# A graph layer on one core: the short slot of the scan moved to tenth place, finer last shares, a shared last normalisation

## The chip, the cores and the metric

The kernel runs on one core of one Trainium2 chip. The core has a matrix engine (TensorE, PE in the profile, with its weight loads as PEld), three engines for elementwise work (VectorE, DVE; ScalarE, ACT; GpSimd, POOL), a queue for transfers (SyncE, SP) and 16 DMA engines that all queues share. Each engine executes its own instructions in the order of the built program, and waits at an instruction until what that one needs is there. The metric is the device time of one execution in microseconds.

## What is computed

```python
def _L0_gnn_ref(x, src, dst, theta_w, theta_b, phi_w, phi_b):
    x_src = x[src]
    x_dst = x[dst]
    theta_x = (x_dst - x_src) @ theta_w.T + theta_b
    phi_x = x_src @ phi_w.T + phi_b
    e = jax.nn.relu(theta_x + phi_x)
    out = jax.ops.segment_max(e, dst, num_segments=x.shape[0])
    return jnp.where(jnp.isfinite(out), out, 0.0)
x = _layernorm(x + _L0_gnn_ref(...), axis=-1)
```

x has 6250 rows of 256 numbers; there are 100,000 edges, sorted by dst. Since relu and the maximum commute with what depends on dst alone, the kernel forms b = x @ (phi - theta).T once for each row, takes for each destination the maximum of b over its sources, adds x @ theta.T and the biases, applies relu, adds x and normalises each row.

## The kernel before

The destinations are split in two parts. Part 1 (the first 1130 nodes) is done by gathering: GpSimd gathers rows of b by edge, VectorE forms running maxima, and the results are stored in a table in device memory, maxima_1. Part 2 is the other 5120 nodes, 40 columns ("tiles") of 128. It is done in two ways at once, and this is the long stage of the kernel.

*The scan.* The 6250 rows of b are cut into 17 slots of up to 383 rows; the last slot has only 122. Each slot is applied to five chunks of 1024 nodes; a pair (slot, chunk) is a part, and there are 85. For a part, SyncE loads a row `want` (L1061, tile pool of 2) that says which row of the slot each node has chosen; VectorE builds the 0/1 mask `hot` for the slot's first block of 128 rows (L1065) and ScalarE those for the other blocks (L1067, L1068); TensorE multiplies the slot's rows (`terms`, a high and a low part) with the masks (L1075), in two halves of one PSUM tile each (`ps_f`, 3 tiles); VectorE takes the maximum into `acc` (L1086), once for each half. A slot of 383 rows has 3 blocks, so 24 matmuls of 512 columns for a part. The short slot has one block, so 8 matmuls, one mask built on VectorE, none on ScalarE, and as before two maxima.

*The list.* Edges that the scan doesn't cover are put in a list. GpSimd gathers their rows of b in 29 groups of 8 steps (gather_2, L512, a tile ring `g` of six), with a pause (L488) after each gather. All of GpSimd's gathers are held in the order in which the code calls them (`in_turn`). VectorE runs through each group with 8 dependent steps (L688), and SyncE stores each group into a second table, maxima_2 (L696).

*The order of the two.* The main loop (L1420 on) takes one list group per turn and calls scan parts (`fetch_parts`) until the blocks that are left fall below a line that SPREAD sets. Within an engine, the order that the code gives is only a priority: a scheduler, working from its own estimates of time while the program is built, lets an instruction go ahead of earlier ones that it believes to be waiting. Exceptions are GpSimd's gathers and, for most of the loop, the L688 steps, which are held behind the latest maximum of the scan (`latest_part`).

*The early share.* A share is a group of up to 8 columns of nodes that is finished together: its x rows are loaded, its maxima gathered (rows_of), TensorE multiplies x with theta, VectorE adds (L1310 for part 2 alone, L1311, L1314), then `normalise` forms the moments on ScalarE (L1328), a small chain on VectorE and a root on ScalarE (L1333, L418 to L424, L1335), scales on ScalarE (L1338) and stores (L1344). One share, LAST, holds the 106 nodes that are left over in part 1: one column. It needs nothing of the list or of the scan's part 2, and is called in the main loop in the turn of list group 26 (L1435 to L1439).

*The end.* After the loop come the 8 other columns of part 1 as one share, then the 40 columns of part 2: four shares of 8 and two of 4. The gathers for part 2 read maxima_2 and wait for all its stores. The pool of the moments `r` has 2 buffers.

Of the kernel before, what the change touches and what calls it, by code (L numbers as in the profile page):

```python
# [40 lines left out]
FP = mybir.dt.float32  # L41
I32 = mybir.dt.int32
# [4 lines left out]
AF = mybir.ActivationFunctionType  # L47
ALU = mybir.AluOpType
# [4 lines left out]
P = 128  # L53
BIG2 = 3.0e38
EPS = 1e-5
STEPS = 8
# [3 lines left out]
TILES = 40  # L60
# [4 lines left out]
KB = 3  # L65
SLOT = 512
DVE_HOTS = 1
SPREAD = 0.97
PAUSE = 160
CHOICE_R = 24  # L70
X_AFTER = 6
# [9 lines left out]
LIST_GROUPS = (LIST + STEPS - 1) // STEPS  # L81
BACK = 34
PAD_WORD = 63 << 14
CARRY_GROUPS = 5
CARRY_AT = 9
FAR = 1000000.0
GENERAL_STEPS = 17
LOWEST = -1.0e30
# [339 lines left out]
def gnn_kernel(ctx: ExitStack, tc: tile.TileContext, x, src, dst, theta_w, theta_b, phi_w, phi_b, out):  # L428
    nc = tc.nc
# [246 lines left out]
    last = {1: None, 2: None}  # L676
    latest_part = [None]

    def run(part, g, n, caps, t0, to, gathers=(), carry_row=None):


        for k in range(n):
            t = t0 + k if part == 1 else LIST_CHUNK - 1 - t0 - k
            if last[part] is not None:
                if t < 0:
                    one = nc.vector.tensor_tensor(g[:, k, :], last[part], carry_row, op=ALU.max)
                else:
                    one = nc.vector.scalar_tensor_tensor(  # L688
                        g[:, k, :], last[part], caps[:, t : t + 1], g[:, k, :], op0=ALU.min, op1=ALU.max
                    )  # L690
                if k < len(gathers):
                    behind_in_order(one, gathers[k], "rows that are there")
                if part == 2 and latest_part[0] is not None:
                    behind_in_order(one, latest_part[0], "VectorE's order")
            last[part] = g[:, k, :]
        nc.sync.dma_start(to, g[:, :n, :])  # L696

    def run_1(i, gathers=()):
        t0, n = groups[i]
# [411 lines left out]
    def list_chunks(ps):  # L1111

        upper_end, scratch, up = (src_w.bitcast(FP)[:, i * P : (i + 1) * P] for i in range(2, 5))
        nc.vector.tensor_copy(upper_end, ps[:, :P])
        nc.vector.tensor_tensor(before, ps[:, P : P + 1], n_list, op=ALU.subtract)
        chunk_0 = work.tile([P, 1], FP, name="chunk_0")
        iota(chunk_0, 0, -BACK, LIST_CHUNK)
        number = work.tile([P, 3], FP, name="number", bufs=1)
        at_edge = chunk_0
        for i in range(3):  # L1120
            nc.vector.tensor_scalar(
                scratch, upper_end, at_edge, None, op0=ALU.is_le, op1=ALU.add, accum_out=number[:, i : i + 1]
            )
            if i == 0:
                nc.vector.tensor_tensor(up, scratch, upper_end, op=ALU.mult)
                nc.vector.tensor_reduce(ends[:, 0:1], up, AX.X, ALU.max)
            nc.vector.scalar_tensor_tensor(up, scratch, FAR, upper_end, op0=ALU.mult, op1=ALU.add)
            nc.vector.tensor_reduce(ends[:, i + 1 : i + 2], up, AX.X, ALU.min)
            at_edge = ends[:, i + 1 : i + 2]
        nc.vector.tensor_scalar(ends, ends, chunk_0, 512.0, op0=ALU.subtract, op1=ALU.min)  # L1130
        nc.vector.scalar_tensor_tensor(number, number, float(OWN_LIST), ends[:, :3], op0=ALU.mult, op1=ALU.subtract)
        nc.vector.tensor_scalar(
            run_start, number, float(OWN_LIST), float((P + 2) * OWN_LIST), op0=ALU.add, op1=ALU.min
        )
        nc.vector.tensor_scalar(bad[:, 7:8], ends[:, 3:4], float(BACK + LIST_CHUNK), None, op0=ALU.is_lt)
        nc.vector.tensor_scalar(bad[:, 8:9], upper_end[:, P - 1 :], float(P * LIST_CHUNK), None, op0=ALU.is_gt)

    def list_places():

        has = work.tile([P, TILES], FP, name="has")  # L1140
        nc.vector.tensor_tensor(has, up_to[:, 1:], up_to[:, :TILES], op=ALU.is_gt)
        place_f = work.tile([P, TILES], FP, name="place_f")
        nc.vector.tensor_scalar(place_f, up_to[:, 1:], before, -1.0, op0=ALU.add, op1=ALU.add)
        chunk_of = work.tile([P, TILES], FP, name="chunk_of")
        floor_of(chunk_of, place_f, LIST_CHUNK)
        nc.vector.tensor_scalar(place_f, up_to[:, :TILES], before, None, op0=ALU.add)
        nc.vector.scalar_tensor_tensor(
            place_f, chunk_of, -float(LIST_CHUNK), place_f, op0=ALU.mult, op1=ALU.add
        )
        step = work.tile([P, TILES], I32, name="step")  # L1150
        group = work.tile([P, TILES], I32, name="group")
        nc.vector.tensor_scalar(
            group, place_f, -float(BACK), None, op0=ALU.is_lt, op1=ALU.add, accum_out=bad[:, 6:7]
        )
        apart = work.tile([P, TILES], FP, name="apart")
        nc.vector.tensor_scalar(apart, place_f, 0.0, float(1 - STEPS), op0=ALU.is_lt, op1=ALU.mult)
        nc.vector.tensor_scalar(apart, apart, float(STEPS), None, op0=ALU.add)
        nc.vector.tensor_scalar(place_f, place_f, -1.0, -1.0, op0=ALU.max, op1=ALU.mult)
        nc.vector.tensor_scalar(step, place_f, float(LIST_CHUNK - 1), 0.0, op0=ALU.add, op1=ALU.max)
        nc.vector.tensor_scalar(group, step, STEPS_BITS, None, op0=ALU.logical_shift_right)  # L1160
        nc.vector.scalar_tensor_tensor(place_f, group, float((P - 1) * STEPS), step, op0=ALU.mult, op1=ALU.add)
        nc.vector.tensor_tensor(chunk_of, chunk_of, apart, op=ALU.mult)
        nc.vector.scalar_tensor_tensor(place_f, chunk_of, 1.0, place_f, op0=ALU.add, op1=ALU.add)
        nc.vector.tensor_tensor(place_f, place_f, has, op=ALU.mult)
        nc.vector.tensor_scalar(place_2, place_f, float(P * LIST), None, op0=ALU.min)

    def list_pieces():
# [35 lines left out]
            nc.vector.copy_predicated(done[:, :n], moves[:, :n], done[:, shift : shift + n])  # L1203
            yield
        done = done[:, :OWN_LIST]
        owner = work.tile([P, 1], I32, name="owner")
        nc.gpsimd.iota(owner, pattern=[[0, 1]], base=0, channel_multiplier=1 << 20)
        nc.vector.tensor_scalar(done, done, (1 << 20) - 1, None, op0=ALU.bitwise_and)
        nc.vector.tensor_tensor(done, done, owner.to_broadcast([P, OWN_LIST]), op=ALU.bitwise_or)
# [28 lines left out]
    def list_carry():  # L1238

        nodes = wide[:, : BACK + LIST_CHUNK]  # L1240
        same = work.tile([P, BACK], FP, name="same_node")
        n_same = work.tile([P, 3], FP, name="n_same")
        nc.vector.tensor_scalar(
            same, nodes[:, :BACK], nodes[:, BACK : BACK + 1], None, op0=ALU.is_equal, op1=ALU.add, accum_out=n_same[:, 0:1]
        )
        step = work.tile([P, 1], I32, name="carry_step")
        group = work.tile([P, 1], I32, name="carry_group")
        nc.vector.tensor_scalar(step, n_same[:, 0:1], -1.0, 0.0, op0=ALU.add, op1=ALU.max)
        nc.vector.tensor_scalar(group, step, STEPS_BITS, None, op0=ALU.logical_shift_right)
        nc.vector.scalar_tensor_tensor(  # L1250
            n_same[:, 1:2], group, float((P - 1) * STEPS), step, op0=ALU.mult, op1=ALU.add
        )
        chunk_1 = work.tile([P, 1], FP, name="chunk_1")
        iota(chunk_1, 0, 1 - STEPS, STEPS)
        nc.vector.tensor_tensor(n_same[:, 1:2], n_same[:, 1:2], chunk_1, op=ALU.add)
        nc.vector.tensor_scalar(n_same[:, 2:3], n_same[:, 0:1], 0.0, None, op0=ALU.is_gt)
        nc.vector.tensor_tensor(n_same[:, 1:2], n_same[:, 1:2], n_same[:, 2:3], op=ALU.mult)
        nc.vector.tensor_scalar(carry_at, n_same[:, 1:2], 0.0, None, op0=ALU.max)
# [14 lines left out]
    def rows_of(part, j0, n, ps_tile):  # L1273
# [8 lines left out]
        maxima, places = (maxima_1, place_1) if part == 1 else (maxima_2, place_2)  # L1282
        for k in range(n):
            gather(m[:, k, :], maxima, places[:, j0 + k : j0 + k + 1])
        totals = work.tile([P, STEPS], FP, name="totals", bufs=3)

        def piece(k):
            w = min(2, n - k)
# [31 lines left out]

    def normalise(part, j0, n, x_f, totals):

        r = work.tile([P, 5, STEPS], FP, name="r")
        mean, var, root, inv, step = (r[:, k, :n] for k in range(5))
        nc.vector.tensor_scalar(mean, totals[:, :n], -1.0 / D, None, op0=ALU.mult)
        for k in range(n):
# [8 lines left out]
        nc.vector.tensor_tensor(mean, mean, inv, op=ALU.mult)  # L1335
        yield
        for k in range(n):
            nc.scalar.activation(  # L1338
                x_f[:, k, :], x_f[:, k, :], AF.Identity, bias=mean[:, k : k + 1], scale=inv[:, k : k + 1]
            )  # L1340
            if k % 2 and k + 1 < n:
                yield
        share = part, j0, n
# [30 lines left out]
                self.step()  # L1374


    parts = [(s, c) for s in range(NS) for c in range(CHUNKS)]
    groups_1 = list(range(X_GROUPS, len(groups)))
    todo = list(range(NT1))

# [41 lines left out]
    for i in range(LIST_GROUPS):  # L1422
# [3 lines left out]
            carry_row = gather_carry()  # L1426
        g, gathers = gather_2(i * STEPS)
        if i:
            run(2, g_before, STEPS, caps_2, (i - 1) * STEPS, maxima_2t[i - 1], gathers)
        g_before = g  # L1430
        while parts and blocks_left() > all_blocks * (1.0 - (i + 1) / (SPREAD * n_groups)):
            fetch_parts(1)
# [12 lines left out]

    ps_end = body.enter_context(tc.tile_pool(name="ps_end", bufs=6, space=PSUM))
    last_shares = [(2, j, STEPS) for j in range(0, TILES - STEPS, STEPS)]
    last_shares += [(2, j, STEPS // 2) for j in (TILES - STEPS, TILES - STEPS // 2)]
    at_end = Shares(lambda: ps_end.tile([P, 2 * D], FP, name="ps_e"))
    for share in [(1, 0, Q1)] + last_shares:  # L1450
        at_end.add(*share)
# [35 lines left out]
```

## Time and profile before

| what | value |
|---|---|
| median of 3 runs (lowest to highest) | 749.13 us (747.54 to 750.01) |
| the profiled execution: time, span | 746.02 us, 744.2 us |
| granted TensorE clock over the span | 0.955 |
| busy share of the span: PE, DVE, ACT, POOL | 87%, 86%, 66%, 81% |
| L1075, matmuls of the scan | x1960, 458.0 us busy |
| L1086, maxima of the scan on VectorE | x160, 193.5 us busy, 1215 ns each |
| L688, steps on gathered rows on VectorE | x376, 180.0 us busy, 479 ns each |
| L512, list gathers on GpSimd | x232, 235.4 us busy, 1015 ns each |
| L488, pauses on GpSimd | x384, 120.4 us busy, 314 ns each |
| L1338, scaling on ScalarE | x49, 25.3 us busy |

A busy share is a mean over stages that have different limits: until about 200 us the tables are prepared, then the scan and the list run together until about 655, then the shares are finished. A matmul's record overlaps with the next one's, so a busy PE is not PE at its peak. What a row of the timeline shows after its names in square brackets is how long the engine had been idle before it, and what ended that idle time.

### The profile page before, as it was taken

Reading aid. Unit: us, or ns where it says so; the run is one execution under the profiler, and the core shown is the slowest. Engines: PE = TensorE matmul, PEld = TensorE weight load, DVE = VectorE, ACT = ScalarE, POOL = GpSimd, SP = SyncE. Lnnn points to the kernel's source line nnn. Section 1 sums busy time; section 2 is a strip of 40 time slices with the busy share of each in tenths; the row PEclk is TensorE's granted clock in tenths of the full one; section 3 lists DMA queues with packets and bytes.
Section 4 is the critical chain, followed back from the end, with each engine's and each line's share of the span. In section 5 each row is a group of like instructions: output and inputs, shape, how many; then the busy total and the mean of one; then the engine's idle time right before and its main releaser. Section 6 shows DMA issues by size and latency. Waiting matters only on the chain.

```text
span 744.2 us, 10255 instructions
## 1 busy us (share of the span) xinstructions
PE 650.4 (87%) x3018; PEld 537.3 (72%) x3018; DVE 641.4 (86%) x1197; ACT 492.7 (66%) x700; POOL 604.9 (81%) x843
## 2 busy tenths in 40 slices
PE   1299999939777999999999999999999999589970
PEld 0288888726556788688888888888888888479970
DVE  6699999999997989598889989889799899768871
ACT  0144444459997777688777877877787775037885
POOL 7788987788887778888888888888888888648840
PEclk9599999959999999999999999999999999999995
DMA  6577745584677787968777777768768777625542
GB/s 207 144 244 244 248 159 193 176 286 151 209 239 256 239 254 231 356 211 267 230 235 223 261 243 251 228 223 251 262 205 261 229 222 250 224 101 180 180 173 116
DMA packets 55895, 164.84 MB, mean 221 GB/s; under 512 B 11835, under 2 KB 19796, under 8 KB 48500
## 3 DMA queue, kind: packets, MB, share of 16 engines
q1 hardware_dynamic: 32344, 98.76, 38.1%
q0 software_dynamic: 20944, 57.62, 27.5%
q10 hardware_dynamic: 2540, 7.69, 2.9%
q8 instruction: 27, 0.44, 0.3%
q14 instruction: 40, 0.33, 0.1%
HBM read 101.08 MB, written 63.74 MB: 221 GB/s over the span
## 4 chain that ended last, share of the span: by engine, by line
PE 52%; ACT 11%; DVE 5%; DMA 5%; POOL 3%; issue 2%; DVEq 0%; ACTq 0%; POOLq 0%; SPq 0%
PE ps_f L1075 49%; DMA want<-chosen_rows 4%; POOL g L512 3%; ACT x_f L1338 3%; ACT squares L1328 3%; ACT hot L1067 2%; ACT hot L1068 2%; DVE acc L1086 2%; PE ps_e L1299 1%; ACT acc L1084 1%; DMA g<-b_rows,src 1%; ACT x_t L1294 1%; DVE g L688 1%; DVE x_f L1314 1%; DVE g L1310 0%
## 5 line engine op out<-in xcount | busy, mean ns | idle before, releaser
L1075 PE MATMUL ps_f<-hot,terms 128*128 128x512 f32 x1960 | 458.0, 395 | 29.0 <-ACT hot L1068 15.6
L1075 PEld LDWEIGHTS ps_f<-hot,terms 128*128 128x128 f32 x1960 | 370.2, 190 | 113.1 <-ACT hot L1068 19.8
L512 POOL DMA_INDIRECT g<-b_rows,list_src x232 | 235.4, 1015 | 39.4 <-issue 35.6
L1067 ACT ACTIVATE hot<-want,minus_row 128x1024 fp32r<-128x1024 f16 x169 | 186.2, 1147 | 92.7 <-PE ps_f L1075 80.2
L1086 DVE TENSOR_TENSOR acc<-acc,ps_f 128x1024 f32<-128x1024 f32 x160 | 193.5, 1215 | 31.9 <-PE ps_f L1075 31.0
L688 DVE SCALAR_TENSOR_TENSOR g<-g,caps 128x256 f32<-128x256 f32 x376 | 180.0, 479 | 8.4 <-DMA g<-b_rows,src 5.2
L1068 ACT ACTIVATE hot<-hot 128x1024 fp32r<-128x1024 f32 x169 | 169.1, 1046 | 0.0
L512 POOL DMA_INDIRECT g<-b_rows,src x98 | 128.0, 1306 | 30.5 <-issue 25.3
L488 POOL IOTA pause<- 128x160 f32 x384 | 120.4, 314 | 5.5
L759 PE MATMUL ps_b<-weights,x_t 128*128 128x256 f32 x388 | 90.5, 388 | 1.3 <-ACT x_t L749 0.5
L759 PEld LDWEIGHTS ps_b<-weights,x_t 128*128 128x128 f32 x388 | 72.9, 192 | 14.4 <-ACT x_t L749 5.0
L512 POOL DMA_INDIRECT g<-in_x_dram,src x48 | 60.3, 1256 | 11.3 <-issue 7.1
L512 POOL DMA_INDIRECT g<-maxima,place x49 | 47.6, 972 | 24.6 <-issue 22.5
L1065 DVE TENSOR_SCALAR hot<-want,row_id 128x1024 fp32r<-128x1024 f16 x76 | 59.8, 788 | 6.4 <-DMA want<-chosen_rows 6.3
L1299 PE MATMUL ps_e<-weights,x_t 128*128 128x256 f32 x192 | 48.5, 380 | 0.3 <-ACT x_t L1294 0.2
L1299 PEld LDWEIGHTS ps_e<-weights,x_t 128*128 128x128 f32 x192 | 32.8, 190 | 3.9 <-ACT x_t L1294 0.8
L1294 ACT COPY x_t<-ps_e 128x512 f32<-128x512 f32 x24 | 13.7, 574 | 32.4 <-PE ps_e L1292 32.4
L762 ACT COPY b_sb<-ps_b 128x512 f32<-128x512 f32 (+1 forms) x25 | 14.4, 578 | 29.8 <-PE ps_b L759 28.0
L762 ACT COPY g<-ps_b 128x512 f32<-128x512 f32 x24 | 14.1, 586 | 29.8 <-PE ps_b L759 27.5
L1338 ACT ACTIVATE x_f<-x_f,r 128x256 f32<-128x256 f32 x49 | 25.3, 590 | 10.8 <-DVE r L1335 10.7
L749 ACT COPY x_t<-ps_xt 128x512 f32<-128x512 f32 (+1 forms) x49 | 26.1, 593 | 0.0
L1328 ACT ACTIVATE squares<-x_f,r 128x256 bf16<-128x256 f32 x49 | 24.2, 499 | 1.6 <-DMA g<-b_rows,list_src 1.0
(266 smaller groups left out, 502.2 us busy)
## 6 DMA issues: line engine op xcount, KB each, us to landing
maxima<-g SPq DMA_DIRECT2D x47, 1024.0 KB
want<-chosen_rows SPq DMA_DIRECT2D x85, 256.0 KB
x_q<-in_x_dram SPq DMA_DIRECT2D x12, 512.0 KB
b_rows<-b_sb ACTq DMA_DIRECT2D x12, 512.0 KB
x_f<-in_x_dram SPq DMA_DIRECT2D x5, 1024.0 KB
out_dram<-x_f SPq DMA_DIRECT2D x5, 1024.0 KB
raw<-b_rows SPq DMA_DIRECT2D x16, 256.0 KB
g<-b_rows,list_src POOLq DMA_INDIRECT x232, 4.3
```

The costliest lines, as they stand in the source:

```text
L488: return nc.gpsimd.iota(t, pattern=[[step, t.shape[1]]], base=base, channel_multiplier=per_partition, allow_small_or_imprecise_dtypes=True,)
L512: in_turn(nc.gpsimd.indirect_dma_start(out=out, out_offset=out_offset, in_=in_, in_offset=in_offset))
L688: one = nc.vector.scalar_tensor_tensor(g[:, k, :], last[part], caps[:, t : t + 1], g[:, k, :], op0=ALU.min, op1=ALU.max)
L759: nc.tensor.matmul(ps[:, h, :], x_t[:, h, k, :], weights[:, k, 0, :], start=(k == 0), stop=(k == KC - 1))
L1065: nc.vector.tensor_scalar(hot[:, b, :], want, row_id[:, b : b + 1], None, op0=ALU.is_equal)
L1067: nc.scalar.activation(hot[:, b, :], want, AF.Abs, bias=minus_row[:, b : b + 1], scale=1.0)
L1068: nc.scalar.activation(hot[:, b, :], hot[:, b, :].bitcast(FP), AF.Relu, bias=1.0, scale=-1.0)
L1075: nc.tensor.matmul(ps[:, w : w + 512], terms[:, part, b, h * P : (h + 1) * P], hot[:, b, w : w + 512], start=(i == 0), stop=(i == n - 1),)
L1086: latest_part[0] = nc.vector.tensor_tensor(to, to, ps, op=ALU.max).ins.name
L1299: nc.tensor.matmul(a[:, i, :], x_t[:, 2 * i + c, :], weights[:, c, 1, :], start=(c == 0), stop=False)
L1328: nc.scalar.activation(squares, x_f[:, k, :], AF.Square, bias=mean[:, k : k + 1], scale=1.0, accum_out=var[:, k : k + 1])
L1338: nc.scalar.activation(x_f[:, k, :], x_f[:, k, :], AF.Identity, bias=mean[:, k : k + 1], scale=inv[:, k : k + 1])
```

## The change

Six edits. The scan takes its slots in another order: the short slot, which was the seventeenth and last, is now the tenth (SHORT_SLOT_AT = 9). SPREAD goes from 0.97 to 0.95, which draws the scan's parts a little forward against the list. The last full list group is stored in two halves, each as soon as its four steps are done. The moments have four buffers (and their totals four instead of three); room for these comes from small tiles of the preparation that now have one buffer instead of two. The last eight columns are finished in shares of 4, 2 and 2 instead of 4 and 4. In the last shares (from column 24 on) every second column is scaled by VectorE instead of ScalarE.

```diff
-SPREAD = 0.97
+SPREAD = 0.95
+SHORT_SLOT_AT = 9
...
-    def run(part, g, n, caps, t0, to, gathers=(), carry_row=None):
+    def run(part, g, n, caps, t0, to, gathers=(), carry_row=None, of_store=STEPS):
...
-        nc.sync.dma_start(to, g[:, :n, :])
+            if k % of_store == of_store - 1 or k == n - 1:
+                a = k // of_store * of_store
+                nc.sync.dma_start(to[:, a : k + 1, :], g[:, a : k + 1, :])
...
-        has = work.tile([P, TILES], FP, name="has")
+        has = work.tile([P, TILES], FP, name="has", bufs=1)
...
-        totals = work.tile([P, STEPS], FP, name="totals", bufs=3)
+        totals = work.tile([P, STEPS], FP, name="totals", bufs=4)
...
-        r = work.tile([P, 5, STEPS], FP, name="r")
+        shared = part == 2 and j0 >= TILES - 2 * STEPS
+        r = work.tile([P, 5, STEPS], FP, name="r", bufs=4)
...
         for k in range(n):
-            nc.scalar.activation(
-                x_f[:, k, :], x_f[:, k, :], AF.Identity, bias=mean[:, k : k + 1], scale=inv[:, k : k + 1]
-            )
+            if shared and k % 2:
+                nc.vector.tensor_scalar(
+                    x_f[:, k, :], x_f[:, k, :], inv[:, k : k + 1], mean[:, k : k + 1], op0=ALU.mult, op1=ALU.add
+                )
+            else:
+                nc.scalar.activation(
+                    x_f[:, k, :], x_f[:, k, :], AF.Identity, bias=mean[:, k : k + 1], scale=inv[:, k : k + 1]
+                )
...
-    parts = [(s, c) for s in range(NS) for c in range(CHUNKS)]
+    in_turn_slots = list(range(NS - 1))
+    in_turn_slots.insert(SHORT_SLOT_AT, NS - 1)
+    parts = [(s, c) for s in in_turn_slots for c in range(CHUNKS)]
...
-            run(2, g_before, STEPS, caps_2, (i - 1) * STEPS, maxima_2t[i - 1], gathers)
+            run(2, g_before, STEPS, caps_2, (i - 1) * STEPS, maxima_2t[i - 1], gathers, of_store=STEPS // 2 if i == LIST_GROUPS - 1 else STEPS)
...
-    last_shares += [(2, j, STEPS // 2) for j in (TILES - STEPS, TILES - STEPS // 2)]
+    last_shares += [(2, TILES - STEPS, STEPS // 2), (2, TILES - STEPS // 2, 2), (2, TILES - 2, 2)]
```

More of the change, by code (lines that the diff above doesn't have):

```diff
@@ L1115, in list_chunks @@
         nc.vector.tensor_tensor(before, ps[:, P : P + 1], n_list, op=ALU.subtract)
-        chunk_0 = work.tile([P, 1], FP, name="chunk_0")
+        chunk_0 = work.tile([P, 1], FP, name="chunk_0", bufs=1)
         iota(chunk_0, 0, -BACK, LIST_CHUNK)
@@ L1138, in list_places @@
     def list_places():
-        has = work.tile([P, TILES], FP, name="has")
+        has = work.tile([P, TILES], FP, name="has", bufs=1)
         nc.vector.tensor_tensor(has, up_to[:, 1:], up_to[:, :TILES], op=ALU.is_gt)
-        place_f = work.tile([P, TILES], FP, name="place_f")
+        place_f = work.tile([P, TILES], FP, name="place_f", bufs=1)
         nc.vector.tensor_scalar(place_f, up_to[:, 1:], before, -1.0, op0=ALU.add, op1=ALU.add)
-        chunk_of = work.tile([P, TILES], FP, name="chunk_of")
+        chunk_of = work.tile([P, TILES], FP, name="chunk_of", bufs=1)
         floor_of(chunk_of, place_f, LIST_CHUNK)
@@ L1149, in list_places @@
         )
-        step = work.tile([P, TILES], I32, name="step")
-        group = work.tile([P, TILES], I32, name="group")
+        step = work.tile([P, TILES], I32, name="step", bufs=1)
+        group = work.tile([P, TILES], I32, name="group", bufs=1)
         nc.vector.tensor_scalar(
@@ L1154, in list_places @@
         )
-        apart = work.tile([P, TILES], FP, name="apart")
+        apart = work.tile([P, TILES], FP, name="apart", bufs=1)
         nc.vector.tensor_scalar(apart, place_f, 0.0, float(1 - STEPS), op0=ALU.is_lt, op1=ALU.mult)
@@ L1205, in list_pieces @@
         done = done[:, :OWN_LIST]
-        owner = work.tile([P, 1], I32, name="owner")
+        owner = work.tile([P, 1], I32, name="owner", bufs=1)
         nc.gpsimd.iota(owner, pattern=[[0, 1]], base=0, channel_multiplier=1 << 20)
@@ L1240, in list_carry @@
         nodes = wide[:, : BACK + LIST_CHUNK]
-        same = work.tile([P, BACK], FP, name="same_node")
-        n_same = work.tile([P, 3], FP, name="n_same")
+        same = work.tile([P, BACK], FP, name="same_node", bufs=1)
+        n_same = work.tile([P, 3], FP, name="n_same", bufs=1)
         nc.vector.tensor_scalar(
@@ L1245, in list_carry @@
         )
-        step = work.tile([P, 1], I32, name="carry_step")
-        group = work.tile([P, 1], I32, name="carry_group")
+        step = work.tile([P, 1], I32, name="carry_step", bufs=1)
+        group = work.tile([P, 1], I32, name="carry_group", bufs=1)
         nc.vector.tensor_scalar(step, n_same[:, 0:1], -1.0, 0.0, op0=ALU.add, op1=ALU.max)
@@ L1252, in list_carry @@
         )
-        chunk_1 = work.tile([P, 1], FP, name="chunk_1")
+        chunk_1 = work.tile([P, 1], FP, name="chunk_1", bufs=1)
         iota(chunk_1, 0, 1 - STEPS, STEPS)
```

## The prediction

> **What bounds the kernel now.** I read the stretches first, then who waited on TensorE, then the timelines where the last parts of the scan end, and last the order in which the two built programs issue on each engine.
>
> ```profile
> 580.00:620.00 40.00, 40.00 (x178) 33.11 (x177) 36.58 (x56) 31.48 (x32) 35.44 (x54) 1.00 0.76 242
> 620.00:655.00 35.00, 25.19 (x109) 19.72 (x108) 30.63 (x52) 7.16 (x10) 22.84 (x36) 0.95 0.59 200
> 655.00:675.00 20.00, 19.76 (x121) 17.96 (x120) 13.34 (x46) 9.41 (x27) 12.58 (x20) 1.00 0.36 119
> 675.00:720.00 45.00, 44.91 (x285) 41.36 (x284) 38.06 (x126) 36.63 (x102) 37.32 (x60) 1.00 0.57 184
> 720.00:744.20 24.20, 1.87 (x12) 1.49 (x10) 6.95 (x36) 15.60 (x49) 0.00 (x0) 0.61 0.33 135
> ```
>
> Columns: stretch, length, busy time of TensorE, its weight loads, VectorE, ScalarE, GpSimd, granted clock, DMA share, GB/s. TensorE is full until 620 and again from 655 to 720. Between, in the short slot's five parts, it idles 9.8 us; the last 24 us belong to ScalarE. VectorE (36.6 of 40) has only some 8% to spare.
>
> ```profile
> 638.02 3.91 PE L1075 MATMUL ps_f<-hot,terms 128*128 128x512 f32 x16 [2.60 <-DVE hot L1065]
> 647.40 5.24 PE L1075 MATMUL ps_f<-hot,terms 128*128 128x512 f32 x16 [5.47 <-DVE hot L1065]
> 654.38 1.09 PE L1292 MATMUL ps_e<-ident,x_f 128*128 128x128 f32 x8 [1.74 <-DVE acc L1086]
> ```
>
> These three gaps are the 9.8 us. The change aims at the first two.
>
> ```profile
> 607.54 0.96 POOL L512 DMA_INDIRECT g<-b_rows,list_src  x1 [0.16 <-issue]
> 608.50 0.29 POOL L488 IOTA pause<- 128x160 f32 x1
> 608.95 1.16 POOL L512 DMA_INDIRECT g<-maxima,place  x1 [0.16 <-DVE acc L1086]
> 610.11 0.28 POOL L488 IOTA pause<- 128x160 f32 x1
> 610.55 0.96 POOL L512 DMA_INDIRECT g<-b_rows,list_src  x1 [0.16 <-DVE g L688]
> ```
>
> GpSimd issues a gather and a pause without a break, about 1.41 us for the pair. The one at 608.95 is the single gather of the early one-column share (L1437 to L1439). It stands behind the gathers of list group 26 (counted from 0) and ahead of group 27's, in both programs.
>
> ```profile
> 575.04 1.21 DVE L1086 TENSOR_TENSOR acc<-acc,ps_f 128x1024 f32<-128x1024 f32 x1
> 576.17 2.04 DVE L688 SCALAR_TENSOR_TENSOR g<-g,caps 128x256 f32<-128x256 f32 x4
> ...
> 624.18 0.41 DVE L1311 TENSOR_TENSOR g<-g,ps 128x256 f32<-128x256 f32 x1
> ```
>
> The L1311 row at 624.18 is VectorE's use of that gather, 15 us after its issue, with no wait. The 575.04 row is the 129th L1086 maximum over a full slot; 21 more follow.
>
> **The change part by part.**
>
> *Short slot tenth.* Its five parts have 8 matmuls each where a full part has 24. The scheduler puts work that nothing holds back into the first idle place it sees on TensorE. Before, that is the short slot at the end; now it is the short slot in the middle. In the built program the early share's transposes, matmuls and its VectorE chain move forward with it: its L1311 add stood among the eight L688 steps of list group 27; now it stands behind those of group 22, ahead of groups 23 to 28, after 139 of 160 maxima (129 of full slots and the short ten). The gather keeps its place behind group 26 on GpSimd, and every GpSimd instruction keeps its order. VectorE takes its instructions in order. So it comes to the add far too early.
>
> When? The 129th full maximum ends its turn at 576.2. Ahead of it now lie the short slot's 40 matmuls, 40 x 0.227 = 9.1 us (0.227: 1364 matmuls in 309.57 us of the chain), and the stall that the short slot brings along, some 6 us: a want buffer is reloaded only after its mask is built and the reload takes about 6 us (640.42 to 646.50 in the chain), so parts four, five and the next full one come late, twice 6 for 9.1 us of matmuls, and ScalarE's masks follow. VectorE arrives at about 591.
>
> The gather: 608.95 plus a landing time of 4.2 us (gathers from 600 to 660 show 3.2 / 4.2 / 5.8, least, median, most) is 613.1. Nothing speeds GpSimd up, and its ring of six tiles is not full (VectorE runs about two groups of 11.9 us behind: group 22 is gathered from 548.37 and first used at 568.36). VectorE stands 22 us. Behind the add in its order wait all remaining maxima, masks and list steps; on ScalarE the share's squares wait for it with the masks of the next part behind them. TensorE can fill three PSUM halves (8.2 us), then stands too. A larger or smaller stall of the short slot changes nothing here: the add cannot run before 613.1.
>
> From 613.1 to the last maximum VectorE has, counted in the new order, with start-to-start times of its rows: 21 maxima x 1.13 = 23.7; 9 masks (L1065) x 0.70 = 6.3; 44 list steps (0.40 alone, 0.51 in runs) x 0.47 = 20.7; the early share 0.33 + 0.47 + 9 small x 0.08 = 1.5; one terms subtraction (L1054) 0.9. That is 53.1. To it comes a wait of 2.6 for ScalarE, which must do the squares (0.7), four masks (4.4) and the cast (0.8) before that subtraction. Sum 55.7, so the last maximum ends at 668.8; before it ended at 654.3 (row 653.11 of VectorE's last maximum plus 1.21). **+14.5 us.** TensorE alone would need 3.0 + 1.2 + 9 x 24 x 0.227 = 53.2, so it is just covered.
>
> *SPREAD 0.95.* All parts are out one part sooner against the list: group 28's first step now comes after 148 full maxima (before 149). Priced inside the count above; 0 by itself.
>
> *Last list group in halves.* The final gathers wait for the last stores (656.2 to 660.81, 4.6 us). Half the bytes in the last store saves between 0 and 2.3; hidden, because the first four pieces after 654.38 use the other table and TensorE reaches the first row that it needs only at 668.03, and stays full after it. 0. If that cover went, the store's 4.6 would move the end directly.
>
> *Four buffers of moments, shares of 4, 2, 2, half on VectorE.* The end now:
>
> ```profile
> 726.49 6.00 ACT L1338 ACTIVATE x_f<-x_f,r 128x256 f32<-128x256 f32 x12 [0.52 <-DVE r L1335]
> ...
> 730.55 0.17 DVE L1325 TENSOR_SCALAR r<-totals 128x4 f32<-128x4 f32 x1 [3.39 <-ACT x_f L1338]
> ...
> 736.39 2.07 ACT L1338 ACTIVATE x_f<-x_f,r 128x256 f32<-128x256 f32 x4 [1.23 <-DVE r L1335]
> ```
>
> The last share's moments wait for a buffer until 730.55 though its rows were ready at 724.7. With four buffers, ScalarE goes on after 726.5 with: 0.4 for what is pulled ahead, 6 x 0.50 (half of twelve), root and last square 0.7, the small chain 1.9 (734.45 to 736.39), 2 x 0.55. That ends at 733.6 instead of 738.46: **-4.9 us.** VectorE's halves are not in the trace: between 0.28 (L822, 128x128) and 0.48 (L688); at most 4 x 0.48 run beside ScalarE's 4 x 0.50, so 0. The last store covers 256 KB instead of 512 KB of a row that takes 5.7 (738.46 to 744.2): saving 0 to 2.9; I take 0, since 1.5 MB of other stores are now close ahead of it. The Trainium skill ("DMA: Bandwidth & Descriptors", the table of two cost components) gives a transfer a fixed 2.0 us plus its bytes at 436 GB/s; by it the halved store would save an estimated 0.6 us, and the sum would be 9.0 instead of 9.6. No row here separates the two.
>
> **Sum.** 14.5 - 4.9 = +9.6 us. The profiled execution took 746.02 (span 744.2), so 755.6; the median shown is 3.1 above it, 749.13, which gives 758.7.
>
> **Rivals.** *The intended effect, faster:* VectorE does not wait at the add. Then the gaps of 2.60 + 5.47 go, the short slot costs some 6 in the middle, a restart like that at 647.40 (5.24 for what took 3.91) goes, the tail gives 4.9: -8.3, so 741. It decides where VectorE is four list groups behind GpSimd (4 x 11.9 us) when it comes to the add; the trace shows 20 for group 22 as above, to which the short slot adds some 15. Against it. *Catching up:* TensorE's floor holds, list steps hide better, the halved store counts in full: about +4, 753. *Starved ring:* GpSimd's groups 27 and 28 now wait for buffers that VectorE frees only at 622 and 638; 28 then lands near 654 against its first use at 666. If those 12 us fail, the end slips by 3 to 6 more: 763. *The tail does not gain* (stores end last): +14.5, 764.
>
> **Chances.** Forecast 0.70, catching up 0.08, starved ring 0.07, tail without gain 0.04, intended effect 0.09, and 0.02 within 0.3% (2.2 us, about what a measurement of this kernel can tell from no change). So faster 0.09, same 0.02, slower 0.89. The forecast's own bounds: landing 3.2 to 5.8, the list steps 0.40 to 0.51, floor of TensorE, tail 3.5 to 7.8: 753.5 to 763.6. With the runs' spread of 1.3 and the neighbours: 751 to 765.
>
> **What would show it.** Right: the early share's add on VectorE near 613 with some 20 us of idle time put down to a DMA; TensorE without matmuls from about 598 to 615; VectorE full from 613 to 670; the first final matmul near 669; ScalarE's last row 12 us after the last matmul instead of 17. Wrong: no wait at that add; or TensorE's gap there, but the final stage starting before 660.

## The result and the profile after

The changed kernel takes 758.64 us (median of 15 runs, 751.36 to 761.50), the kernel before 749.27 us beside it (15 runs, 745.50 to 755.50): ratio 1.0124, 95% interval 1.0098 to 1.0150. So it is 9.4 us slower. Ratios, here and below, are formed from each kernel's faster runs alone, so they need not equal the quotient of the medians. The profiled execution took 760.86 us (span 759.0), 14.8 more than that of before.

First the stretches, with the same columns as before:

```profile
600.00:615.00 15.00, 15.00 (x68) 12.43 (x67) 11.33 (x17) 9.73 (x10) 13.32 (x21) 1.00 0.73 237
615.00:640.00 25.00, 21.09 (x86) 16.54 (x85) 17.63 (x35) 17.29 (x20) 19.99 (x31) 0.93 0.53 161
640.00:670.00 30.00, 30.00 (x134) 24.82 (x134) 29.41 (x45) 22.37 (x23) 15.49 (x24) 1.00 0.73 250
690.00:735.00 45.00, 45.00 (x288) 41.71 (x287) 37.51 (x131) 34.74 (x100) 38.22 (x61) 1.00 0.57 185
735.00:759.00 24.00, 7.78 (x46) 6.70 (x44) 15.83 (x69) 17.61 (x54) 4.03 (x8) 0.72 0.42 158
```

TensorE stops for 3.9 us between 615 and 640, VectorE idles more, and from 640 on both are full. TensorE's timeline, in the short slot and at the end of the scan:

```profile
461.33 3.94 PE L1078 MATMUL ps_f<-hot,terms 128*128 128x512 f32 x16 [1.60 <-DVE hot L1068]
469.41 5.35 PE L1078 MATMUL ps_f<-hot,terms 128*128 128x512 f32 x16 [4.14 <-DVE hot L1068]
477.48 4.80 PE L1078 MATMUL ps_f<-hot,terms 128*128 128x512 f32 x20 [2.72 <-DVE hot L1068]
...
623.10 50.89 PE L1078 MATMUL ps_f<-hot,terms 128*128 128x512 f32 x216 [3.91 <-DVE r L1337]
675.36 1.09 PE L1295 MATMUL ps_e<-ident,x_f 128*128 128x128 f32 x8 [1.38 <-DVE acc L1089]
```

The gaps that stood at 638 and 647 have moved to 461, 469 and 477, together 8.5 us; a new one of 3.91 stands at 623, and the final matmuls begin at 675.36 (before 654.38). GpSimd and VectorE around the early share:

```profile
617.25 0.95 POOL L513 DMA_INDIRECT g<-maxima,place  x1 [0.16 <-issue]
618.21 0.28 POOL L489 IOTA pause<- 128x160 f32 x1
621.16 0.95 POOL L513 DMA_INDIRECT g<-b_rows,list_src  x1 [2.67 <-DVE r L1329]
```

```profile
347.48 1.21 DVE L1089 TENSOR_TENSOR acc<-acc,ps_f 128x1024 f32<-128x1024 f32 x1
...
611.33 1.21 DVE L1089 TENSOR_TENSOR acc<-acc,ps_f 128x1024 f32<-128x1024 f32 x1
620.00 0.42 DVE L1314 TENSOR_TENSOR g<-g,ps 128x256 f32<-128x256 f32 x1 [7.46 <-DMA g<-maxima,place]
...
674.10 1.21 DVE L1089 TENSOR_TENSOR acc<-acc,ps_f 128x1024 f32<-128x1024 f32 x1
```

The 620.00 row is the early share's add (L1311 before). VectorE came to it at 612.5 and waited 7.46 us for the gather issued at 617.25; before, the gather was issued at 608.95, the add ran at 624.18 and nothing waited. The first L1089 row is the 40th of the 160 maxima, the last row the 160th. ScalarE at the end:

```profile
747.54 3.20 ACT L1347 ACTIVATE x_f<-x_f,r 128x256 f32<-128x256 f32 x6
750.64 0.19 ACT L420 ACTIVATE r<-r 128x2 f32<-128x2 f32 x1
...
751.82 0.20 ACT L420 ACTIVATE r<-r 128x2 f32<-128x2 f32 x1 [0.50 <-DVE r L425]
752.05 0.60 ACT L1347 ACTIVATE x_f<-x_f,r 128x256 f32<-128x256 f32 x1
753.43 0.60 ACT L1347 ACTIVATE x_f<-x_f,r 128x256 f32<-128x256 f32 x1 [0.79 <-DVE r L1339]
```

No wait for a buffer of the moments is left. The last matmul ends at 742.79, ScalarE at 754.03, the span at 759.0: 16.2 us after the last matmul, against 22.3 before.

Set by stages, the two profiles differ so: at the 40th maximum the changed kernel is 14.2 us later (347.5 against 333.3), from there to the 160th it takes 326.6 against 319.8, the final matmuls take 67.5 in both, the end 6.1 less. The first difference was in no step of the prediction.

### The profile page after: what moved, and what is told of

Read it like the earlier page. It is cut to its first block, busy times and chain, and to the rows that moved or that the text cites. A ratio compares the mean times of both kernels' runs of the same rounds, so it can differ in the third digit from the quotient of the medians.

```text
span 759.0 us, 10272 instructions
## 1 busy us (share of the span) xinstructions
PE 659.8 (87%) x3018; PEld 542.7 (72%) x3018; DVE 645.8 (85%) x1214; ACT 488.6 (64%) x693; POOL 613.9 (81%) x843
## 5 line engine op out<-in xcount | busy, mean ns | idle before, releaser
L1078 PE MATMUL ps_f<-hot,terms 128*128 128x512 f32 x1960 | 468.2, 400 | 39.3 <-ACT hot L1071 12.4
L1078 PEld LDWEIGHTS ps_f<-hot,terms 128*128 128x128 f32 x1960 | 376.2, 193 | 127.6 <-ACT hot L1071 17.3
L513 POOL DMA_INDIRECT g<-b_rows,list_src x232 | 238.5, 1028 | 42.0 <-issue 36.5
L1089 DVE TENSOR_TENSOR acc<-acc,ps_f 128x1024 f32<-128x1024 f32 x160 | 193.8, 1214 | 34.0 <-PE ps_f L1078 33.1
L513 POOL DMA_INDIRECT g<-b_rows,src x98 | 138.1, 1409 | 30.5 <-issue 25.4
L489 POOL IOTA pause<- 128x160 f32 x384 | 116.5, 303 | 5.4
L762 PEld LDWEIGHTS ps_b<-weights,x_t 128*128 128x128 f32 x388 | 72.4, 191 | 14.8 <-ACT x_t L752 5.4
L513 POOL DMA_INDIRECT g<-maxima,place x49 | 47.1, 961 | 33.8 <-DMA maxima<-g 14.2
L765 ACT COPY b_sb<-ps_b 128x512 f32<-128x512 f32 (+1 forms) x25 | 14.5, 579 | 29.6 <-PE ps_b L762 25.9
L1347 ACT ACTIVATE x_f<-x_f,r 128x256 f32<-128x256 f32 x41 | 21.6, 592 | 7.4 <-DVE r L1339 7.2
L1297 ACT COPY x_t<-ps_e 128x512 f32<-128x512 f32 x24 | 13.7, 575 | 19.5 <-PE ps_e L1295 19.5
```

Source lines behind the costliest of these rows:

```text
L489: return nc.gpsimd.iota(t, pattern=[[step, t.shape[1]]], base=base, channel_multiplier=per_partition, allow_small_or_imprecise_dtypes=True,)
L513: in_turn(nc.gpsimd.indirect_dma_start(out=out, out_offset=out_offset, in_=in_, in_offset=in_offset))
L762: nc.tensor.matmul(ps[:, h, :], x_t[:, h, k, :], weights[:, k, 0, :], start=(k == 0), stop=(k == KC - 1))
L1078: nc.tensor.matmul(ps[:, w : w + 512], terms[:, part, b, h * P : (h + 1) * P], hot[:, b, w : w + 512], start=(i == 0), stop=(i == n - 1),)
L1089: latest_part[0] = nc.vector.tensor_tensor(to, to, ps, op=ALU.max).ins.name
L1347: nc.scalar.activation(x_f[:, k, :], x_f[:, k, :], AF.Identity, bias=mean[:, k : k + 1], scale=inv[:, k : k + 1])
```

## The experiments

They ran on four other chips, where the kernel before takes 799 to 817 us, with runs of one kernel up to 4% apart; whole times decide little there. So three figures are read from each trace besides: the *middle* (start of the 40th to start of the 160th maximum), VectorE's wait at the early add, and the *end* (last matmul to the end of the span). Line numbers of the held kernel are up to 5 higher than the changed one's.

**First set: parts of the change, and the wait taken away.** Theory W: the wait in the early add sets the end. M: the short slot costs the time by being in the middle. L: the tiles' new places delay the preparation.

*The early share held behind list group 25:*

```diff
+            if last[part] is not None:
+                latest_step[0] = one.ins.name
...
-            nc.vector.tensor_tensor(some, some, a[:, :w, :], op=ALU.add)
+            one = nc.vector.tensor_tensor(some, some, a[:, :w, :], op=ALU.add)
+            if share == LAST:
+                behind_in_order(one, latest_step[0], "rows that are there")
```

> The changed kernel, with one edit: on VectorE the early one-column share's add is ordered behind the last step of list group 25, so that it comes after 153 maxima and not after 139. Theory W (the wait of that add for its row sets the end): the wait is gone; what is left is the short slot's price in the middle (21.5 us in the profile of the changed kernel) against its price at the end before (19.5) and the tail's gain of 5 to 6, so about 745. Rival M (the short slot in the middle costs the time by itself, the add only waits for time that is lost anyway): 756 to 759, as the changed kernel. Rival L (the preparation runs later because small tiles and moments lie differently): 756 to 759.

*The changed kernel with the short slot last:*

```diff
-SHORT_SLOT_AT = 9
+SHORT_SLOT_AT = 16
```

> The changed kernel with the short slot at the end again (SHORT_SLOT_AT = 16), all else as changed. W: the early add stands after 148 maxima, no wait; tail gain 5 to 6 and nothing else: 743 to 745. M: 743 to 745 too. L: 751 or more, since the tiles lie as in the changed kernel.

*The kernel before with the move alone:*

```diff
-    parts = [(s, c) for s in range(NS) for c in range(CHUNKS)]
+    in_turn_slots = list(range(NS - 1))
+    in_turn_slots.insert(9, NS - 1)
+    parts = [(s, c) for s in in_turn_slots for c in range(CHUNKS)]
```

> The kernel before with the short slot moved to tenth place and nothing else. The early add stands after 137 maxima. W: the wait without the tail's gain: 749 + 14.5 = 763 to 765. M: the same 763 to 765. L: 749 to 752, since no tile lies otherwise than before.

*The end's edits alone (the changed kernel without the move, the spread and the halves):*

```diff
-SPREAD = 0.95
+SPREAD = 0.97
-SHORT_SLOT_AT = 9
+SHORT_SLOT_AT = 16
...
-            run(2, g_before, STEPS, caps_2, (i - 1) * STEPS, maxima_2t[i - 1], gathers, of_store=STEPS // 2 if i == LIST_GROUPS - 1 else STEPS)
+            run(2, g_before, STEPS, caps_2, (i - 1) * STEPS, maxima_2t[i - 1], gathers)
```

> The changed kernel without the slot's move, with SPREAD 0.97 and the last list group stored whole: what is left is four buffers of moments, one buffer for small tiles, shares of 4, 2, 2, half of the scaling on VectorE. W and M: 749 - 5.5 = 743 to 745, the last scaling ending 11 to 12 us after the last matmul. L: 750 or more, with the first list gather some 10 us later than before.

Measured against the kernel before (798.99 us): held 801.97, ratio 1.0046 (0.9977 to 1.0115); short slot last 797.56, 1.0006 (0.9941 to 1.0071); move alone 817.33, 1.0257 (1.0195 to 1.0318); end alone 792.24, 0.9935 (0.9866 to 1.0003). The move alone costs some 18 us by the medians (21 by the ratio), which W and M foresaw in kind and L did not. The short slot last, at 797.56, lies between what W and M expected (a ratio of some 0.993) and what L did (1.003 or more). Between W and M the whole times leave it open: the held kernel lies between what each expected. The add of the move alone, in VectorE's timeline:

```profile
632.87 1.21 DVE L1086 TENSOR_TENSOR acc<-acc,ps_f 128x1024 f32<-128x1024 f32 x1
649.97 0.42 DVE L1311 TENSOR_TENSOR g<-g,ps 128x256 f32<-128x256 f32 x1 [15.89 <-DMA g<-maxima,place]
```

and TensorE behind it:

```profile
624.72 16.03 PE L1075 MATMUL ps_f<-hot,terms 128*128 128x512 f32 x70
653.08 7.11 PE L1075 MATMUL ps_f<-hot,terms 128*128 128x512 f32 x23 [12.33 <-DVE r L1333]
```

Here the wait is 15.9 us, and TensorE, which has room for three halves in PSUM, stands 12.3 of them. Once VectorE goes on, GpSimd, TensorE and ScalarE all follow. The wait is not the whole price here: the stretch from the 40th maximum to the 160th is 23.5 us longer than before (table below), and VectorE idles again behind the add, 2.95, 4.08 and 2.15 us, the second time for a `want` row. What makes these waits was not tested.

**Second set: the kernel before as its own control, the changed one, held, and short slot last.**

> The kernel before, unchanged, as its own control. The profile of the changed kernel showed the first list gather at 287.4 us against 277.2 in the profile before, and the 40th maximum 14.2 us later, long before anything that the change is meant to touch. Theory L (the changed layout of tiles delays the preparation): the first list gather of this run is at 276 to 279 again, and that of the changed kernel near 287. Theory V (the preparation's end varies from run to run): this run's first list gather may be anywhere from 277 to 290, with the whole time moving by less than that. Ratio to the kernel before 1.000 within 0.003 in both.

> The changed kernel unchanged, so that the next two kernels stand against it on one chip. Ratio 1.010 to 1.015 (757 to 760 where the kernel before takes 749). Theory W (VectorE waits in the early share's add for its gathered row): the add idles 7 to 22 us, put to a DMA, and the last maximum ends 55 to 56 us after that row lands. Theory L: first list gather near 287; theory V: not tied to that.

> As the changed kernel, but the early share's work is ordered behind list group 25, so that VectorE doesn't stand in its add before its row can be there. The wait measured in the profile of the changed kernel was 7.5 us. Theory W: that much comes back, ratio 1.002 to 1.004 (751 to 752 where before takes 749). Theory M (the short slot in the middle costs the time by itself, the wait only fills what would be lost anyway): nothing comes back, ratio 1.010 to 1.013 (757 to 759).

> As the changed kernel, but the short slot is put back to the end; what is left of the change is the halves, the spread, the buffers of moments and the finer tail. Theories W and M both: only the tail's gain is left, 6.2 us by the profile of the changed kernel (16.1 us from the last matmul to the end against 22.3), ratio 0.992 (743 where before takes 749). Theory L: the later preparation stays, some 5 to 10 us, so that the ratio is 0.999 to 1.006.

The unchanged kernel came out at 0.9822 (0.9743 to 0.9901) of itself, so this chip's whole times and even their intervals prove nothing: changed 0.9895 (0.9802 to 0.9989), held 0.9990 (0.9918 to 1.0061), short slot last 0.9809 (0.9716 to 0.9902). Taken over the control's own ratio, the changed kernel is at 0.9895 / 0.9822 = 1.007, short slot last at 0.999 and held at 1.017, worse than changed, which neither W nor M foresaw. The traces tell more; they stand in the table below. The changed kernel's wait came out at 6.8 us, a little under the 7 to 22 expected, and from the landing to the end of the last maximum it took 57.3 us, where 55 to 56 were expected. The held kernel's add in this set has no wait in front of it:

```profile
684.96 0.42 DVE L1317 TENSOR_TENSOR g<-g,ps 128x256 f32<-128x256 f32 x1
```

**Third and fourth set: short slot last and held again; changed and the end alone again.**

> As the changed kernel with the short slot at the end. Its instructions stand in the order of the kernel before on every engine as far as the 54th maximum, and its tiles lie as in the changed kernel. Tail gain 6.0 us (16.2 us from the last matmul to the end against 22.2), middle 0 (40th to 160th maximum 319 to 321 us, as before). Theory V (the preparation's end differs from execution to execution, not from kernel to kernel): ratio 0.990 to 0.994 (742 to 745 where before takes 749). Theory L (where the tiles lie makes the preparation later, by the 7 to 8 us that the stages of the changed kernel leave unexplained): ratio 1.000 to 1.004.

> As the changed kernel, its early share held back behind list group 25. Middle (40th to 160th maximum) 320 to 324 us, so 0 to 4 more than before, against 327 to 329 in the changed kernel; tail gain 6.0. Theory V: ratio 0.992 to 0.997 (743 to 747 where before takes 749). Theory L: 7 to 8 us more, ratio 1.002 to 1.007 (751 to 754).

> The changed kernel unchanged, beside the next one on the same chip. Middle (40th to 160th maximum) 327 to 332 us against 320 before, of it 7 to 12 us VectorE's wait in the early share's add; tail 6.0 us shorter. By these two alone ratio 1.001 to 1.008; what was measured at first was 1.0124 (1.0098 to 1.0150). Theory V (which of two courses the preparation takes is chance, with one gather of some 10 us near 180 us in the later one): a profile with that gather has its first list gather 8 to 10 us later than one without it. Theory L (the changed kernel always takes the later course): the gather of some 10 us is there.

> The kernel before with the buffers of moments, the shares of 4, 2, 2 and VectorE's half of the last normalisations, and nothing else of the change. Middle 320 to 321 us as before, no wait at the early share's add, tail 6.0 us shorter. Theories W and V: ratio 0.990 to 0.994. A theory that the tail's gain is taken back by the stores that then come close together: 0.997 to 1.000, with the store behind the last row longer than 5.7 us.

Measured: short slot last 0.9938 (0.9883 to 0.9993), held 1.0018 (0.9945 to 1.0091), changed 1.0020 (0.9963 to 1.0078), end alone 0.9983 (0.9927 to 1.0039). All stages together:

| kernel | middle, us | wait at the early add, us |
|---|---|---|
| before (profile before; control) | 319.8; 320.3 | none |
| changed (first profile; second, fourth set) | 326.6; 328.8; 329.6 | 7.5; 6.8; 7.5 |
| held (first, second, third set) | 323.6; 320.6; 324.0 | none |
| short slot last (first, second, third set) | 319.0; 320.2; 320.0 | none |
| end alone (first, fourth set) | 320.5; 319.2 | none |
| move alone | 343.6 | 15.9 |

The middle repeats within 3.4 us on five chips, and by it W has the larger share: the changed kernel's mean is 328.3, the held one's 322.7, before's 320.1. So 5.6 of 8.3 us go with the wait, and some 2.6 stay with the slot's place. That split is rough. On the one chip on which all three were profiled (second set) the middles are 328.8, 320.6 and 320.3, and next to nothing stays with the place; in the held kernel's other two traces it is 3.5 and 3.9 against the mean of before. The end is 22.3 and 22.0 us in before's two profiles, 16.2 in all three of the changed kernel, 15.8 to 16.0 in the held one's, and 16.5 to 17.0 in the five with the short slot last (the end alone among them), where 6.0 less than before had been expected and 5.0 to 5.8 came.

The held kernel's whole time does not show what its middle gives back: 1.0046, 0.9990 and 1.0018 where 0.992 to 0.997 was expected. Its final matmuls, which fall in the chips' own disturbance (see the last section), take 95.3, 99.8 and 98.5 us, against 94.5 and 93.8 in the changed kernel and 98.0 in the control; where the rest went stays open.

The end alone in the fourth set, at 0.9983, fell where the rival had put it (0.997 to 1.000: the close stores take the end's gain back), but its interval holds the 0.990 to 0.994 of W and V as well. In its trace 5.2 us of the end's gain are there; the rest behind the last row is 5.7 us, no longer than before.

**The preparation.** The first list gather is issued at 277.2 in the profile before and 287.4 in the changed kernel's. The built programs issue in the same order on every engine up to the 54th maximum, GpSimd in the same order throughout. The gathers near 180 us, in GpSimd's timelines; first the control, which is the kernel before:

```profile
178.31 2.15 POOL L512 DMA_INDIRECT g<-b_rows,src  x1 [0.30 <-issue]
180.76 9.82 POOL L512 DMA_INDIRECT g<-b_rows,src  x1 [0.30 <-DMA g<-b_rows,src]
190.88 4.12 POOL L512 DMA_INDIRECT g<-b_rows,src  x1 [0.30 <-issue]
```

the changed kernel's first profile:

```profile
178.16 2.15 POOL L513 DMA_INDIRECT g<-b_rows,src  x1 [0.30 <-issue]
180.62 9.75 POOL L513 DMA_INDIRECT g<-b_rows,src  x1 [0.30 <-issue]
190.68 7.37 POOL L513 DMA_INDIRECT g<-b_rows,src  x1 [0.30 <-issue]
```

the held kernel in the third set, whose tiles lie as the changed kernel's:

```profile
180.23 3.74 POOL L513 DMA_INDIRECT g<-b_rows,src  x1 [0.30 <-issue]
184.28 3.05 POOL L513 DMA_INDIRECT g<-b_rows,src  x1 [0.30 <-issue]
187.63 2.24 POOL L513 DMA_INDIRECT g<-b_rows,src  x1 [0.30 <-issue]
```

and the profile before:

```profile
179.85 3.75 POOL L512 DMA_INDIRECT g<-b_rows,src  x1 [0.30 <-DMA g<-b_rows,src]
183.91 3.02 POOL L512 DMA_INDIRECT g<-b_rows,src  x1 [0.30 <-issue]
```

The same gather takes 3.7 us or 9.8. There are two courses, one with gathers of over 5 us in this stretch and one without. The kernel before has shown both, and so have the held kernel (in the first set its gathers took 5.75 and 7.41 from 183.94 on) and the changed one (in the second set none is over 5). In its strict form, that the new places of the tiles always make the preparation later, L is refuted. The expectations' theory V says that the course is chance. Short slot last in the third set, at 0.9938 (0.9883 to 0.9993), is what V expected, and L's 1.000 to 1.004 lies outside. But V's sign, that a list behind a gather of some 10 us begins 8 to 10 us later, failed in the fourth set: the changed kernel has such a gather and the end alone has not (there they take 5.7 and 7.4), and their lists begin at 311.7 and 311.8. The control's list, at 315.1, began later than either theory had put it (276 to 279, 277 to 290). Whether the tiles' places make the later course more frequent is open: all three profiles of the changed kernel began their list late, but two of them fall on chips where every kernel's list began late.

## Why the prediction was right, and where it was not

The forecast was 758.7 us, the median 758.64. That agreement is luck: the sum's term for the early add was too large, its term for the end a little small, and some 7 us came from a stage that it left out.

*The scheduler takes the early share forward and VectorE waits in its add for a gather that stays where it was:* right. The wait is in all four profiles of kernels with the moved slot and the early share free, and in none of the ten others.

*Its size, 22 us: the step that failed.* It was 7.5. Counted from the 40th maximum, VectorE was to arrive at 591 - 333.3 = 257.7 and arrived at 612.5 - 347.5 = 265.0; the row was to land at 613.1 - 333.3 = 279.8 and landed at 620.0 - 347.5 = 272.5. Of the first 7.3 us, 6.4 are the short slot: "some 6" of stall was put on 9.1 of matmuls, 15.1 in all, and it took 21.5 (from the maximum at 456.3 to that at 480.5, less the 2.7 of a usual step; 21.5 to 24.4 in the other traces). At the end it had taken 19.5. So the short slot's gaps do not vanish in the middle; three stand there instead of two. The second 7.3 us are GpSimd: in this execution it began its list 4 us earlier against the maxima than in the profile before (60.1 us ahead of the 40th, before 56.1), kept pace by 2 us better (329.8 us from the first list gather to the early one, before 331.8), and the landing took 2.7 us instead of 4.2. Only these second 7.3 us bear on the time: as the prediction itself says, a longer stall changes nothing while the row is late. What failed in the cost is thus the landing, which was taken over from the profile before as if GpSimd's distance from the scan were fixed. A wait is the difference of two long chains, and an error of 3% in either is its whole size.

*The +14.5 us that follow from it* shrank with it: by the middles +6.8 in the first profile, +8.3 in the mean. With the landing 7.3 us nearer, 14.5 becomes 7.2. The step inside it was all but exact: 55.7 us were counted from the landing to the end of the last maximum, and it took 55.3 (620.0 to 675.3), then 57.3 and 55.3 in the second and fourth set.

*Sign of TensorE without matmuls from 598 to 615:* wrong. It stood 3.9 us at 623. With a wait of 7.5, PSUM's room for 8.2 us of matmuls covers most of it; that the early add then holds VectorE is seen on VectorE, not on TensorE.

*The halves and the spread at 0:* not contradicted. With the short slot last, the halves and the spread left in, the middles are 319.0 to 320.2. One by one they were not run.

*The end, -4.9 us:* right in kind, 6.1 measured in the first pair. The four buffers took the wait at 730.55 away, and ScalarE's last row ends 11.2 us after the last matmul, 12 having been named. VectorE's halves run beside ScalarE's. From the last matmul to that row the two profiles differ by 5.4 us, against the 4.9 of the term; the rest lies behind the row, where the span ends 5.0 us later instead of 5.7 (759.0 - 754.03; the profile before 744.2 - 738.46). That is not the smaller store, whose saving the prediction put at 0. The Trainium skill ("DMA: Bandwidth & Descriptors", the table of two cost components) gave an estimate of 0.6 us for it, and the runs do not bear it out: the last packet of the last store ends 2.5 us behind the last row in both profiles, and in the five traces with the same last store and the short slot last the span ends 5.6 to 5.8 us behind that row, as before. What ends sooner in the changed and the held kernel's traces (4.9 to 5.1) stays open.

*The sum.* By stages +8.3 - 6.0 = +2.3 us, and the median says +9.4 (7.3 to 11.2). On the chip of the fourth set the changed kernel stood at 1.0020 (0.9963 to 1.0078), which +2.3 of 801 fits. The rest on the first chip, some 7 us, lies before the 40th maximum as far as the pair of profiles shows, where it is 14.2; that pair lies 14.8 apart, the medians only 9.4. The later course of the preparation in most runs of the changed kernel could make that, but it is not shown; no run of the experiments fell on a chip like the first.

*The rivals.* The intended effect (741) needed no wait at the add. The held kernel shows how far it was away even so: without the wait its middles are 0.5 to 3.9 us longer than before's mean, where -3.4 would have been (the gaps of 2.60 and 5.47 and the restart of 1.3 gone, 6 paid). The starved ring was there in the trace (GpSimd idles 10.2 us at 655.67 for a buffer) and cost nothing that can be seen, since the last stretch kept to its 55.3.

*A better kernel.* Leaving the short slot last keeps 5 to 6 us of the end's gain and has no wait. On these chips that is 0.9935 (0.9866 to 1.0003) and 0.9983 (0.9927 to 1.0039) with the end's edits alone, and with the halves and the spread 1.0006 (0.9941 to 1.0071) and 0.9938 (0.9883 to 0.9993), the second set, whose control came out at 0.98, left out. By its middle and its end it is 5 to 6 us better than the kernel before; by whole times that is likely but not settled.

## What to carry to other kernels

A gap that is filled by moving work is also a place into which a scheduler puts other work; look up which instructions follow it, and whether the transfers they need have moved too, since on an engine that works in order one early instruction holds everything behind it. Where whole times are noisy, count from a row that both traces have (here the 40th maximum) and compare stage by stage. A wait found as the difference of two long chains should be given with the errors of both, and a sum that meets the median is no proof of its terms.

## What the runs showed of the hardware

*A GpSimd gather beside long VectorE work.* The gather that takes 3.75 us in one execution and 9.75 in another runs while VectorE executes rows of 0.3 to 1.9 us without a break; the list's gathers later on mostly take 0.95, beside VectorE's maxima and list steps. Within 15 us one course has issued four gathers more, and 100 us later it is 10 us ahead. The Trainium skill ("SBUF — State Buffer", the box on VectorE blocking DMA) says that while VectorE runs an operation in a two-port mode, GpSimd cannot write the descriptors of a transfer that it issues. That could lengthen these gathers. But the end of any one VectorE row is at most 1.9 us away, VectorE begins more than ten rows within the gather of 9.75, and both courses run beside the same rows; no run here took VectorE's work away to test it, so the cause is open.

*A stop of all three compute engines.* On the four other chips ScalarE, VectorE and TensorE stop at about the same time while the list is prepared, whatever the kernel: the longest stop of a trace is 18 to 34 us on ScalarE, 10 to 29 on VectorE and 9 to 33 on TensorE. On the first chip it is 7.2 at most. The control's timelines, VectorE and TensorE:

```profile
271.32 2.35 DVE L1086 TENSOR_TENSOR acc<-acc,ps_f 128x1024 f32<-128x1024 f32 x2 [28.84 <-remote]
```

```profile
272.60 4.89 PE L1075 MATMUL ps_f<-hot,terms 128*128 128x512 f32 x12 [31.90 <-DVE acc L1086]
```

The profile names no releaser within the core ("remote"). GpSimd is busy for 21.8 of the 33 us from 237 to 270. In the final stage such waits come again, up to 8.85 us each; the control's final matmuls take 98 us instead of 67.5. These two make some 59 of the 69 us by which the control's span is longer than that of the profile before. Their cause is open.
